# Statistics of the second image: 32 pieces of 512 pixels in three pairs a period, in place of 64 pieces of 256 spread over it

## The chip, the cores and the metric

The kernel runs on one core of a Trainium2 chip. The metric is the device time of one launch in microseconds (us), as the median of several runs. Profiles show one execution of the program; DVE is VectorE, ACT ScalarE, PE TensorE, POOL GpSimd, and SP the engine whose queue issues nearly all the DMAs here.

## What is computed

The input `x` is float32, 2 images x 512 channels x 64 x 64 pixels. There are two layers with a residual each:

```python
x = x + _L0_conv_ref(_gn(x), ...)   # group norm, then deformable convolution
x = x + _L1_conv_ref(_gn(x), ...)   # group norm, then attention over 4096 pixels
```

Layer 0 normalizes each image over 32 groups of channels (`_gn`: mean and variance of a group over all its pixels). A projection of the normalized image is the source that is sampled. A depthwise 3x3 convolution, a layer norm over channels and a GELU give, by a matmul, offsets and masks; bilinear samples at the offset places, weighted by the masks, go through an output matmul. So nothing of the second image can be projected before the mean and the variance of that whole image are known: this is what `image_stats` supplies.

## The kernel before

An image is cut into 8 chunks of 512 pixels (`CH = 512`, `NCH = 8`, 8 rows of 64), the channels into 4 blocks of 128 partitions (`KB = 4`). Layer 0 is a software pipeline over 16 chunks (`NSEQ = 16`, 8 of each image). The stages are generators, and each `yield` ends a step:

- `project(i)` (L724) reads chunk i of x into `raw` (three of the four loads in its first step, L737), normalizes it on ACT into `xn` (L748), multiplies it by the input weights (`pq`, L758) and writes the rows to DRAM (`xt<-xj`, L766).
- `features(i)` (L771): the first of nine taps of the depthwise convolution on ACT (L783), the other eight of each channel block on DVE (L788, 32 instructions), the sum over blocks on POOL (L796), the mean over channels by a matmul (`p_mean`, L801), the subtraction on DVE (L806), squares, the root of the variance on ACT (`rstd`, L818), then the norm: its reciprocal (L820) and the product (L821) on DVE, and GELU on ACT (L825).
- `weights(i)` (L833): offsets and masks (`po` on PE L842, `o` on DVE L847), then the bilinear weights on DVE (L859 to L890), a copy on ACT (L893) and transposes.
- `sample(i)` (L919): matmuls (`pb`, `pa`) on patches of projected pixels, the output matmul `py` (L969), and its evacuation on DVE: an addition (L974), a bn_stats for layer 1 (L975) and a write of the chunk (`wx<-res`, L976). At the end of each half of `pa`, `fetch` (L905 to L916) issues eight loads of patches for the next chunk (L914, 192 KB each).
- `image_stats(1)` (L697): one step per piece of the second image. It keeps up to three loaded pieces in `xraw` (three buffers): each step first issues loads until three pieces are under way, then takes the oldest for a `bn_stats` (L713) on DVE. The load of piece k+2 is therefore issued in the step of piece k. After a channel block's last piece, at the start of the following step, comes a `bn_aggr` (L715). The group norm's few instructions follow (`group_norm_steps`, L599).

The order of all this is written out by hand in `period` (L998 to L1050), which is called 16 times inside `tc.manual_schedule()` (L1087): on every engine, and in SP's queue of DMAs, instructions stand in the order in which `period` resumes the generators. Its letters: `y` is `sample(i-1)` in its output part, `v` and `w` the weights of chunks i and i+1, `f` the features of i+2, `m` `sample(i)`, `g` the features of i+3 (its ACT tap only), `p` the projection of i+3, and `more` one step of `image_stats(1)`. A period starts with `p(); y(); v(4); f(4); y()`: raw loads, first output matmul, transposes, four taps, evacuation. Then four rounds of `m(2); w(); more(); f(taps); w(); more()` do the other 28 taps. The mean follows, outputs, and the step `f()` of the norm (L820, L821) after `p(); y(2)`. The tail of the period has the products of `weights`, the projection's matmuls and writes, and five more `more()`. A period so has 13 steps of `more`, five periods 65: the 64 pieces and the last `bn_aggr`. At i = 5 (`NCH - 3`), `run(later)` (L1091) finishes the statistics, since period 5 projects chunk 8, the first of the second image.

Image 0's statistics use the same function ahead of the periods (with pieces of 512, from tiles that hold the whole image).

Layer 1 (attention) follows and takes the rest of the span.

Of the kernel before, what the change touches and what calls it, by code (L numbers as in the profile page):

```python
# [9 lines left out]
F32 = mybir.dt.float32  # L10
# [7 lines left out]
P = 128  # L18
NB = 2
C = 512  # L20
KB = C // P
H = W = 64
S = H * W
# [7 lines left out]
CH = 512  # L31
NCH = S // CH
# [498 lines left out]
def kernel(ctx: ExitStack, tc: tile.TileContext, t_in: dict, out: bass.AP):  # L531
# [7 lines left out]
    nc.vector.tensor_reduce(al[:, 1:2], al[:, 0:1], AX.X, ALU.max, apply_absolute_value=True)  # L539
    nc.vector.memset(al[:, 0:1], 1.0 / SCORE_MAX)  # L540
    window_path(tc, t_in, out, far, sums)


# [27 lines left out]
def window_path(ctx: ExitStack, tc: tile.TileContext, t_in: dict, out: bass.AP, far: bass.AP, sums: bass.AP):  # L571
    nc = tc.nc
    x_v = t_in["x"].rearrange("n (cb p) h w -> n p cb (h w)", p=P)
# [25 lines left out]
    def group_norm_steps(mv, k, small, psum, result):  # L599

        p1 = psum.tile([P, CH], F32, tag="mm", name="gn_p1")
        nc.tensor.matmul(p1[:, : 2 * k], gmat, mv.rearrange("p k s -> p (k s)"), start=True, stop=True)
        yield
        gm = small.tile([P, k, 2], F32, name=f"gn_gm{k}")
        nc.vector.tensor_copy(gm.rearrange("p k s -> p (k s)"), p1[:, : 2 * k])
        d = small.tile([P, k], F32, name=f"gn_d{k}")
        nc.vector.tensor_sub(d, mv[:, :, 0], gm[:, :, 0])
        nc.vector.tensor_mul(d, d, d)
        yield
        p2 = psum.tile([P, CH], F32, tag="mm", name="gn_p2")  # L610
        nc.tensor.matmul(p2[:, :k], gmat, d, start=True, stop=True)
        yield
        var = small.tile([P, k], F32, name=f"gn_var{k}")
        nc.vector.tensor_add(var, gm[:, :, 1], p2[:, :k])
        nc.scalar.activation(var, var, AF.Sqrt, bias=eps)
        yield
        sc = small.tile([P, k], F32, name=f"gn_sc{k}")
        nc.vector.reciprocal(sc, var)
        bi = small.tile([P, k], F32, name=f"gn_bi{k}")
        nc.vector.scalar_tensor_tensor(bi, gm[:, :, 0], -1.0, sc, ALU.mult, ALU.mult)  # L620
        result += [sc, bi]
# [8 lines left out]
    with ExitStack() as l0:  # L630
        wp = l0.enter_context(tc.tile_pool(name="w0w", bufs=1))
        io = l0.enter_context(tc.tile_pool(name="w0io", bufs=1))
        cv = l0.enter_context(tc.tile_pool(name="w0conv", bufs=1))
        sm = l0.enter_context(tc.tile_pool(name="w0small", bufs=1))
# [10 lines left out]
        img = [bt.rearrange("p g q d -> p (g q d)")[:, h * S : (h + 1) * S] for h in range(2)]  # L645
# [51 lines left out]
        def image_stats(n):  # L697

            mv = sm.tile([P, KB, 2], F32, name="gn_mv")
            size = CH if n == 0 else CH // 2  # L700
            pieces, ahead = deque((kb, h) for kb in range(KB) for h in range(S // size)), deque()
            for kb in range(KB):
                st = sm.tile([P, 16, 6], F32, name="gn_st")
                for h in range(S // size):
                    if n == 0:
                        t = img[kb][:, h * size : (h + 1) * size]
                    else:
                        while len(ahead) < 3 and pieces:
                            k2, h2 = pieces.popleft()
                            ahead.append(io.tile([P, size], F32, name="xraw", bufs=3))  # L710
                            nc.sync.dma_start(ahead[-1], x_v[n, :, k2, h2 * size : (h2 + 1) * size])
                        t = ahead.popleft()
                    nc.vector.bn_stats(st[:, h, :], t)  # L713
                    yield
                nc.vector.bn_aggr(mv[:, kb, :], st[:, : S // size].rearrange("p a b -> p (a b)"))  # L715
            yield
            result = []
            yield from group_norm_steps(mv, KB, sm, ps, result)
            sc, bi = result
            gn[n] = [sm.tile([P, KB], F32, name=f"gn_{k}{n}") for k in ("scale", "bias")]  # L720
            nc.vector.tensor_copy(gn[n][0], sc)
            nc.vector.tensor_copy(gn[n][1], bi)
# [184 lines left out]
        def fetch(i, s):  # L907

            if i >= NSEQ:
                return  # L910
            n, ch = divmod(i, NCH)
            t = io.tile([P, PX, C], F32, name="patch", bufs=2)
            for p in range(PX):
                nc.sync.dma_start(  # L914
                    t[:SN, p, :], xt_d[n][ch * ROWS + PR * s : ch * ROWS + PR * s + SY, PC * p : PC * p + SX, :]
                )  # L916
            patches[i, s] = t
# [61 lines left out]
        def run(*generators):  # L979
            for gen in generators:  # L980
                for _ in gen:
                    pass
# [15 lines left out]
        def period(y, v, m, w, f, g, p, more):  # L998

            p()
            y()
            v(4)
            f(4)
            y()
            for taps in (9, 7, 6, 6):
                m(2)
                w()  # L1010
                more()
                f(taps)
                w()
                more()
            w()
            m()
            w()
            m()
            f()
            y()  # L1020
            f()
            m()
            p()
            w(2)
            y(2)
            w()
            m()
            p()
            f()
            w(2)  # L1030
            p()
            y(2)
            f()
            y()
            m()
            p()
            more()
            for k, steps in enumerate((1, 2, 2, 2)):
                p()
                w(steps)  # L1040
                if k == 0:
                    f()
                p()
                more()
                if k < 3:
                    m()
                if k == 0:
                    f()
                if k == 2:
                    g()  # L1050
            w()
# [17 lines left out]
        def output_bias():  # L1069
# [8 lines left out]
            yield  # L1078

        run(image_stats(0), project(0), value_weights(), features(0), project(1))  # L1080
        v = Chain(weights, 0)
        v(23)
        run(features(1), project(2), output_bias())
        fetch(0, 0)
        fetch(0, 1)
        later, y, f = image_stats(1), Chain(sample, NSEQ), Chain(features, 2)
        with tc.manual_schedule():  # L1087
            f()
            for i in range(NSEQ):
                if i == NCH - 3:  # L1090
                    run(later)  # L1091
                w, m, g = Chain(weights, i + 1), Chain(sample, i), Chain(features, i + 3)
                period(y, v, m, w, f, g, Chain(project, i + 3), lambda: next(later, None))
                y, v, f = m, w, g
            y.rest()

# [4 lines left out]
    with ExitStack() as l1, tc.manual_schedule():  # L1101
# [8 lines left out]
        with ExitStack() as at, ExitStack() as inner:  # L1110
# [69 lines left out]
            mv = bnp.tile([P, NB * KB, 2], F32, name="mv2")  # L1180
# [107 lines left out]
            for n in range(NB):  # L1288
# [38 lines left out]
                for qb in range(NCH):  # L1327
                    acc = {}
                    for kp in range(NPAIR + 2):
# [23 lines left out]
                        if kp < NPAIR:  # L1353
                            v = ready.pop(0)
                            e, tt, _ = made[qb, kp]
                            ops = operands(lambda k: e[:, k, :], tt)
                        else:
                            v = w7[:, kp - NPAIR]
# [17 lines left out]
                    a = [acc[j].rearrange("p (cb q) -> p cb q", cb=2) for j in range(6)]  # L1376
# [156 lines left out]
```

## Time and profile before

| | us |
|---|---|
| median of three runs | 3704.61 (3700.99 to 3706.11) |
| the profiled execution | 3707.44 |
| its span, first to last instruction | 3705.6 |
| first tap of period 1 to that of period 2, of 2 to 3, of 3 to 4 | 75.3, 75.9, 74.7 |

| engine | busy us | share of the span |
|---|---|---|
| PE | 3417.9 | 92% |
| DVE | 2345.8 | 63% |
| ACT | 1304.1 | 35% |
| POOL | 291.0 | 8% |

The mean granted TensorE clock is 0.968 of full speed. The profile is read in several views: the page's 40 slices of the span with busy tenths; the waits, in which a line gives the instruction that waited, the one that released it, the total in us, the count and the longest; the timeline, in which each line is a start, a duration, an engine, a source line and an operation, with the idle time before it in brackets; the issues on SP's queue (SPq), which show when a DMA was issued and not when it landed; and the chain that ended last, followed back from the end, in which a DMA has the time from its issue to its landing.

In the traced execution the 64 pieces of `xraw` run on DVE from 175.1 to 533.0 us, 403 to 429 ns each, 25.8 us in all with their overlap. Image 0's 32 pieces of 512 take 675 to 694 ns each.

### The profile page before, as it was taken

The numbers are of one execution on the slowest core, as the hardware profiler recorded it, in microseconds if no ns is written. First come the engines' busy times: TensorE is split into PE (matmuls) and PEld (weight loads), VectorE is DVE, ScalarE is ACT, GpSimd is POOL, SyncE is SP. The second block draws the span as 40 slices with busy tenths as digits, with TensorE's granted clock in tenths as the row PEclk, the third lists the DMA queues.
The fourth block names the chain that finished last, engine by engine and source line by source line (L and its number), as shares of the span: only waits on it lengthen the run. The fifth ranks groups of instructions, "written<-read, shape, count | busy, mean of one in ns | idle before, by whom it ended". The sixth has DMA issues, their size and how long they took to land.

```text
span 3705.6 us, 39010 instructions
## 1 busy us (share of the span) xinstructions
PE 3417.9 (92%) x15151; PEld 2433.8 (66%) x15151; DVE 2345.8 (63%) x3575; ACT 1304.1 (35%) x1691; POOL 291.0 (8%) x190
## 2 busy tenths in 40 slices
PE   4689998999998799999999999999999999999990
PEld 1355555555555477777777777777777777777770
DVE  5798989999996475545554554567455455545544
ACT  2476777787886321111111111221111111111114
POOL 2112111212111030000000000022000000000000
PEclk9789999999999899999999999999999999999995
DMA  7233442342432444334334333444433333243349
GB/s 240 63 98 114 135 137 83 115 133 83 127 109 78 142 157 171 126 129 139 123 108 163 122 125 130 140 155 169 149 121 111 122 138 111 101 149 121 111 162 389
DMA packets 180181, 500.06 MB, mean 135 GB/s; under 512 B 22640, under 2 KB 64368, under 8 KB 170512
## 3 DMA queue, kind: packets, MB, share of 16 engines
q1 hardware_dynamic: 176496, 473.34, 37.5%
q10 hardware_dynamic: 3456, 24.12, 1.7%
q8 instruction: 121, 1.98, 0.2%
q14 instruction: 76, 0.62, 0.0%
q0 software_dynamic: 32, 0.00, 0.0%
HBM read 406.09 MB, written 91.29 MB: 134 GB/s over the span
## 4 chain that ended last, share of the span: by engine, by line
PE 75%; DVE 15%; DMA 4%; ACT 2%; SPq 1%; issue 1%; POOL 1%; ACTq 0%; DVEq 0%; POOLq 0%
PE acc L1364 41%; DVE conv L788 8%; PE pS L1211 7%; PE p L1402 7%; PE py L969 5%; PE pq L758 4%; PE pa L949 4%; PE pv L1251 3%; PE pk L1305 1%; PE p_mean L801 1%; DVE pk L885 1%; DVE aw L890 1%; DMA patch<-xt 1%; DMA out<-ct 1%; DVE o L847 1%
## 5 line engine op out<-in xcount | busy, mean ns | idle before, releaser
L1364 PE MATMUL acc<-e,v 128*128 128x256 f32 x3072 | 768.2, 386 | 0.0
L1215 ACT ACTIVATE e<-pS 128x1024 f32<-128x1024 f32 x256 | 262.0, 1024 | 1386.4 <-PE pS L1211 1313.0
L1364 PE MATMUL acc<-tt,v 128*128 128x256 f32 x3072 | 748.2, 380 | 0.5 <-DMA v<-wv 0.5
L1364 PEld LDWEIGHTS acc<-e,v 128*128 128x128 f32 x3072 | 566.5, 190 | 233.2 <-issue 165.3
L1364 PEld LDWEIGHTS acc<-tt,v 128*128 128x128 f32 x3072 | 582.4, 190 | 91.2 <-issue 10.6
L1218 DVE TENSOR_TENSOR t<-e 128x256 f32<-128x256 f32 x256 | 108.8, 425 | 761.1 <-ACT e L1215 761.1
L788 DVE SCALAR_TENSOR_TENSOR conv<-xn,L_conv_dw_w_sb,conv 128x504 f32<-128x504 f32 (+1 forms) x512 | 399.7, 795 | 48.5 <-ACT conv L783 36.5
L1228 DVE TENSOR_TENSOR tot<-tot,e 128x512 f32<-128x512 f32 x480 | 330.1, 688 | 8.3
L949 PEld LDWEIGHTS pa<-bt,patch 96*128 96x128 f32 x2048 | 251.8, 197 | 63.1 <-issue 39.4
L1211 PE MATMUL pS<-q,kq 64*128 64x512 f32 x1024 | 289.0, 641 | 0.0
L949 PE MATMUL pa<-bt,patch 96*128 96x128 f32 x2048 | 255.3, 281 | 9.3 <-ACT dT L960 5.8
L935 ACT COPY bt<-pb 96x1024 f32<-96x1024 f32 x124 | 234.2, 2001 | 58.9 <-PE pb L930 58.9
L758 PE MATMUL pq<-L_conv_in_w_sb,xn 128*128 128x512 f32 x512 | 236.3, 605 | 4.3 <-ACT xn L748 4.3
L969 PE MATMUL py<-dT,L_conv_out_w_sb 128*128 128x512 f32 x512 | 238.0, 610 | 0.0
L1402 PE MATMUL p<-t,v 128*128 128x256 f32 x1024 | 231.4, 382 | 1.7 <-DMA v<-wv 1.7
L1402 PEld LDWEIGHTS p<-t,v 128*128 128x128 f32 x1024 | 192.1, 190 | 48.5 <-issue 21.2
L960 ACT COPY dT<-pa 32x256 f32<-32x256 f32 x496 | 179.5, 362 | 89.8 <-PE pa L949 80.9
L842 PE MATMUL po<-om_w_pg,feat 128*128 128x432 f32 x512 | 203.4, 542 | 0.0
L969 PEld LDWEIGHTS py<-dT,L_conv_out_w_sb 128*128 128x128 f32 x512 | 99.3, 197 | 119.6 <-issue 115.5
L758 PEld LDWEIGHTS pq<-L_conv_in_w_sb,xn 128*128 128x128 f32 x512 | 94.1, 194 | 109.5 <-issue 93.0
L842 PEld LDWEIGHTS po<-om_w_pg,feat 128*128 128x128 f32 x512 | 93.0, 191 | 90.5 <-issue 89.4
L1211 PEld LDWEIGHTS pS<-q,kq 64*128 64x128 f32 x1024 | 77.1, 184 | 84.9 <-issue 84.9
(203 smaller groups left out, 3731.2 us busy)
## 6 DMA issues: line engine op xcount, KB each, us to landing
v<-wv SPq DMA_DIRECT2D x252, 768.0 KB
patch<-xt SPq DMA_DIRECT2D x256, 192.0 KB
v<-wv SPq DMA_DIRECT2D x256, 128.0 KB
wv<-v SPq DMA_DIRECT2D x32, 896.0 KB
xt<-xj SPq DMA_DIRECT2D x128, 128.0 KB
res<-in_x SPq DMA_DIRECT2D x64, 256.0 KB
wx<-res SPq DMA_DIRECT2D x64, 256.0 KB
xq<-wx SPq DMA_DIRECT2D x16, 1024.0 KB
```

The lines of the kernel that those rows point to most:

```text
L758: nc.tensor.matmul(pq, xn[:, kb, 1 + 2 * t : 3 + 2 * t, :].rearrange("p r c -> p (r c)"), in_w[:, kb, :], start=(kb == 0), stop=(kb == KB ...
L788: nc.vector.scalar_tensor_tensor(dst, src, wt, dst, ALU.mult, ALU.add)
L842: nc.tensor.matmul(po[:, : 3 * GP], f[:, kb, t * P : (t + 1) * P], om_w[:, kb].rearrange("p a k g -> p (a k g)"), start=(kb == 0), stop=(k ...
L935: copy(bt[:SN].rearrange("s g q d -> s d (g q)")[:, d0 : d0 + 4, :], pb[:SN])
L949: nc.tensor.matmul(pa[:, p], xp[:SN, p, cb * P : (cb + 1) * P], bt[:SN, 4 * cb : 4 * cb + 4, PX * s + p, :], start=True, stop=True,)
L960: copy(dst, src)
L969: nc.tensor.matmul(py, out_w[:, kb, cb * P : (cb + 1) * P], dT[:, kb, :], start=(kb == 0), stop=(kb == KB - 1))
L1211: nc.tensor.matmul(pS[:, h, :], kq[r, 2 * (kp // 4) + h, c0 : c0 + P], qs[qb][r, :], start=True, stop=True)
L1215: nc.scalar.activation(e.rearrange("p a q -> p (a q)"), pS.rearrange("p h q -> p (h q)"), AF.Exp)
L1228: nc.vector.tensor_add(tots[qb], tots[qb], e2[:, h, :])
L1364: nc.tensor.matmul(acc[j][:, cb * HQ : (cb + 1) * HQ], v[:, j, cb * P : (cb + 1) * P], ops[j], start=(kp + cb == 0), stop=(kp + cb == NPAI ...
L1402: nc.tensor.matmul(p7[:, cb * HQ : (cb + 1) * HQ], v7[:, cb * P : (cb + 1) * P], t3, start=(k + cb == 0), stop=(k + cb == NPAIR + 2),)
```

## The change

`image_stats(1)` uses pieces of 512 pixels (256 KB a load in place of 128 KB), 32 in place of 64, still with three buffers. `more` takes a number of pieces. The 13 single steps of a period go; there are three pairs in their place: ahead of the first four taps, between these and the output's evacuation, and ahead of the norm. That is 6 steps a period and 30 in five, so `run(later)` at period 5 has two pieces and a `bn_aggr` more to do. Image 0's statistics are the same as before.

```diff
         def image_stats(n):
 
             mv = sm.tile([P, KB, 2], F32, name="gn_mv")
-            size = CH if n == 0 else CH // 2
-            pieces, ahead = deque((kb, h) for kb in range(KB) for h in range(S // size)), deque()
+            pieces, ahead = deque((kb, h) for kb in range(KB) for h in range(NCH)), deque()
             for kb in range(KB):
-                st = sm.tile([P, 16, 6], F32, name="gn_st")
-                for h in range(S // size):
+                st = sm.tile([P, NCH, 6], F32, name="gn_st")
+                for h in range(NCH):
                     if n == 0:
-                        t = img[kb][:, h * size : (h + 1) * size]
+                        t = img[kb][:, h * CH : (h + 1) * CH]
                     else:
                         while len(ahead) < 3 and pieces:
                             k2, h2 = pieces.popleft()
-                            ahead.append(io.tile([P, size], F32, name="xraw", bufs=3))
-                            nc.sync.dma_start(ahead[-1], x_v[n, :, k2, h2 * size : (h2 + 1) * size])
+                            ahead.append(io.tile([P, CH], F32, name="xraw", bufs=3))
+                            nc.sync.dma_start(ahead[-1], x_v[n, :, k2, h2 * CH : (h2 + 1) * CH])
                         t = ahead.popleft()
                     nc.vector.bn_stats(st[:, h, :], t)
                     yield
-                nc.vector.bn_aggr(mv[:, kb, :], st[:, : S // size].rearrange("p a b -> p (a b)"))
+                nc.vector.bn_aggr(mv[:, kb, :], st.rearrange("p a b -> p (a b)"))
             yield
...
             p()
             y()
             v(4)
+            more(2)
             f(4)
+            more(2)
             y()
             for taps in (9, 7, 6, 6):
                 m(2)
                 w()
-                more()
                 f(taps)
                 w()
-                more()
             w()
...
             p()
             y(2)
+            more(2)
             f()
             y()
             m()
             p()
-            more()
             for k, steps in enumerate((1, 2, 2, 2)):
                 p()
                 w(steps)
                 if k == 0:
                     f()
                 p()
-                more()
                 if k < 3:
                     m()
...
         later, y, f = image_stats(1), Chain(sample, NSEQ), Chain(features, 2)
+
+        def more(pieces):
+
+            for _ in range(pieces):
+                next(later, None)
+
         with tc.manual_schedule():
...
-                period(y, v, m, w, f, g, Chain(project, i + 3), lambda: next(later, None))
+                period(y, v, m, w, f, g, Chain(project, i + 3), more)
```

## The prediction

> **What bounds the kernel now.** I read the page's 40 slices first, to find the stage the change touches. A digit is the busy tenth of 92.6 us.
>
> ```profile
> PE   4689998999998799999999999999999999999990
> DVE  5798989999996475545554554567455455545544
> ```
>
> DVE is at 9 tenths up to about slice 12, PE from slice 14 on. The change touches only layer 0's first six periods, where both are close to full, so I went to the waits of DVE between 171 and 545 us (periods 0 to 4, and the start of 5).
>
> ```profile
> DVE conv L788 <- ACT conv L783: 10.5, 4, 8.0
> DVE rstd L820 <- ACT rstd L818: 10.2, 5, 3.1
> DVE gn_st L713 <- DMA xraw<-in_x: 8.7, 5, 2.9
> DVE res L974 <- PE py L969: 5.7, 4, 1.4
> ```
>
> These are the three places of the new calls (first taps L788, evacuation L974, norm L820), and a wait of the statistics on their own loads. Third, DVE's timeline where period 1 begins (start, duration, in brackets the idle time before).
>
> ```profile
> 236.76 0.43 DVE L713 BATCH_NORM_STATS2 gn_st<-xraw 128x6 f32<-128x256 f32 x1 [0.82 <-DMA xraw<-in_x]
> 238.58 3.09 DVE L788 SCALAR_TENSOR_TENSOR conv<-xn,L_conv_dw_w_sb,conv 128x504 f32<-128x504 f32 x4 [1.39 <-ACT conv L783]
> 243.09 0.75 DVE L974 SCALAR_TENSOR_TENSOR res<-py,L_conv_out_b_sb,res 128x512 f32<-128x512 f32 x1 [1.42 <-PE py L969]
> ...
> 244.81 6.85 DVE L788 SCALAR_TENSOR_TENSOR conv<-xn,L_conv_dw_w_sb,conv 128x504 f32<-128x504 f32 x9
> ...
> 254.13 0.43 DVE L713 BATCH_NORM_STATS2 gn_st<-xraw 128x6 f32<-128x256 f32 x1 [1.62 <-DMA xraw<-in_x]
> ```
>
> The four first taps end at 241.67; a piece issued at the first `more()` of the period is waited for at 254.13. Fourth, SP's issues over the same stretch, and the chain's step through it.
>
> ```profile
> 236.64 0.54 SPq L711 DMA_DIRECT2D xraw<-in_x  x1
> 237.24 0.42 SPq L941 DMA_DIRECT2D res<-in_x  x1
> 237.75 5.67 SPq L914 DMA_DIRECT2D patch<-xt  x8
> 243.52 1.14 SPq L766 DMA_DIRECT2D xt<-xj  x2
> 244.75 0.53 SPq L711 DMA_DIRECT2D xraw<-in_x  x1
> 245.40 2.40 SPq L737 DMA_DIRECT2D raw<-in_x  x3
> 248.63 0.33 SPq L976 DMA_DIRECT2D wx<-res  x1
> ```
> ```profile
> 242.77 6.99 DMA patch<-xt
> 249.77 4.33 DMA xraw<-in_x
> 254.13 0.43 DVE gn_st L713
> ```
>
> This is the view that decides. At a period's edge SP issues eight patch loads (192 KB each), two xt writes and three raw loads (320 KB each); the last patch has landed at 249.75, and the piece issued behind all that needs 4.33 us more, where the piece issued at 234.35 took 2.39. The chain that sets the end runs through it.
>
> **What the Trainium skill says.** *DMA: Bandwidth & Descriptors*, section Queues, rings and completion order: SP's transfers share one row of rings, and each DMA engine takes descriptors in ring order. The trace agrees: 4.33 against 2.39 us. *Perfetto Trace Analysis*, section DMA Instruction — HWDGE: the profiled stretch of an issue is not the movement of the data; so I take landings from the chain, not from the 0.33 us of an issue. *VectorE: DVE Perf Modes*, section on the TRN2 errata: every instruction on SBUF operands pays a fixed cost (58 cycles at 0.96 GHz, 60 ns), so larger pieces pay it less often. The trace agrees: eight 512-wide bn_stats of image 0 take 4.84 us, 0.605 each; a pair of 256-wide ones 0.74, a pitch of 0.333. Two halves cost 0.666, one whole 0.605: 0.061 saved.
>
> **The change part by part.**
>
> *Size of the piece.* 64 x 0.333 = 21.3 us become 32 x 0.605 = 19.4: 2 us of DVE in all. The transfers double to 256 KB, the total is the same.
>
> *Number of pieces.* Before, 13 `more()` a period, 65 by the end of period 4: 64 pieces and the last bn_aggr. After, 6 a period: 30. The last two pieces and a bn_aggr fall to `run(later)` at the head of period 5. There, DVE has shed four trailing pieces of period 4 (4 x 0.335 = 1.3 us) and gets 2 x 0.605 = 1.2; the group norm then waits 4.7 us on ACT L615 anyway. I take 0, bounds -1 and +1.
>
> *Issue order, the heart of it.* Each resumption tops `ahead` up to three, then uses the oldest: piece k issues the load of k+2. Call a period's pairs A (before the first taps), B (after four taps), C (before the norm). A's two resumptions issue B's loads, B's issue C's, C's issue the next A's. So A and C arrive early: C's loads have 40 us, the next A's some 20. B's loads are issued at the head of the period, behind eight patches, two xt and three raw, and are wanted four taps later. Before, the load issued at the first `more()` was used two resumptions on, nine taps and an evacuation later, and still came 1.34 to 2.87 us late.
>
> *When B lands.* Let T0 be the start of the first tap (238.58, 313.91, 389.82, 464.54 for periods 1 to 4). The reference load landed just before its bn_stats, at 254.13, 330.71, 405.81, 479.82: T0 + 15.6, 16.8, 16.0, 15.3, mean 15.9. Bytes behind the patches up to there: xt 0.26, xraw 0.13, raw 0.98, wx 0.26, xraw 0.13 MB, 1.77 in all. After, to the end of b1: xt 0.26, raw 0.98, b1 0.26, 1.5 MB; to the end of b2 1.77, the same. The DMA moves about 0.385 MB/us there (356 to 397 GB/s in the slices before 250), so b1 lands 0.7 before b2. Three of the trailing xraw issues stood in SP's chain ahead of the patches, and two of them between an xt and a res, at 0.59 each: the patches start about 1 us earlier. b2: T0 + 14.9; b1: T0 + 14.2.
>
> *What that costs.* Four taps end at T0 + 3.1. DVE then idles to T0 + 14.2, 11 us, since the instruction at its head waits. Queued behind it: the evacuation and its bn_stats (1.4), 28 taps, the om additions, the sum for the mean. Behind the evacuation waits the x1 write on SP, behind the taps POOL and then PE's p_mean. b2 ends at T0 + 15.5; evacuation and stats 1.4, nine taps 6.8, addition 0.5 bring it to T0 + 24.2. Before, the same point, third `more()` included, is at T0 + 16.2. Loss 8.0. Five later `more()` before the mean go: 5 x 0.335 = 1.7. Net 6.3 a period, 25 us over four periods.
>
> *Is it given back later?* From p_mean to the norm the chain is PE (py, pa, py, pa: 277.04 to 289.6), then ACT, queued in order behind p_mean; it moves as a whole. Pair C costs 1.2 and lies in the wait for rstd (0.9 to 3.1), I take 0; uncovered it would be 1.2 x 4 = 5 us. Pair A (1.2) takes the place of two of the trailing pieces and of the 0.5 to 1.4 us wait on ACT's L783; T0 is set by ACT, so 0, both ways at most 1.3 a period. The `c2` load waits on SP for bn_stats of b1; behind it only the x1 write, which waits for the same DVE: 0.
>
> *Period 0.* Its first three loads are issued at 140.6, long before use. Eight `more()` go (2.7 us), B costs 1.2, C 0.3 beyond a wait of 0.9: -1.2. But b2 waits for a1's buffer and may stand behind the xt writes, which end at 176.3; with 2.4 + 0.35 for landing it comes at 179, DVE wants it at 175.3: up to +3.8. I take +1, bounds -1.2 and +2.6.
>
> Sum: 25 + 1 = +26 us. The profiled execution took 3707.4 us (span 3705.6, 1.8 around it), the median is 3704.6, the runs spread over 5. On the profiled one: 3733; on the median: 3730.6, given as 3730.
>
> **Rivals.**
>
> *B's loads pass the bulk.* The patches keep the DMA engines only half busy (digits 4 to 6 in that stretch), so b1 and b2 might land 2.7 us after their issue, at about T0 + 11 and T0 + 11.7. Then the nine taps end at T0 + 21: loss 4.8 - 1.7 = 3.1 a period, 12 in all: 3717. Against it: the same traffic held the reference load for 4.33 us.
>
> *Faster: the pairs do fit into the gaps.* If b1 and b2 were there when the four taps end, DVE would reach the point of comparison at T0 + 3.1 + 1.2 + 1.4 + 6.8 + 0.5 = T0 + 13.0 in place of 16.2, and save 1.7 more: 4.9 a period, 20 in four, 1 in period 0: 3684. It decides from the landing of b2: sooner than T0 + 8.6 is a gain, later a loss. Against it: the eighth patch, ahead in the same queue, lands at T0 + 11.2.
>
> *Worse: nothing of the 1 us on SP is gained, and C and A lie open.* Each period 1 + 1.2 + 1 more: +13: 3743.
>
> *No change to speak of:* the idle DVE lets PE and ACT run ahead, so that the waits of 10.2 (rstd) and 5.7 (py) go, together with the early landing: 3707. Against it: what PE does between p_mean and rstd stands behind p_mean.
>
> **How the numbers follow.** Main case 0.74, 3730, own range 3720 to 3741. Early landing 0.11, 3717. Worse 0.05, 3743. No change 0.05, 3707. Faster 0.05, 3684. The range 3712 to 3744 leaves out the last two and the tails. 0.2% is 7.4 us, about what a measurement of this kernel can tell from no change. Faster by more (under 3697): 0.05. Within: 0.05 and 0.03 of the early landing's lower side, 0.08. Slower: 0.87.
>
> **What would show it.** In periods 1 to 4 DVE should wait some 11 us in front of the first bn_stats after four taps, released by DMA xraw; the wait of L713 on xraw rises from 8.7 to about 44 to 48 us. The waits of L974 on PE (5.7) should vanish, those of L820 shrink by C. A period from first tap to first tap goes from 75.3 to about 81.6 us; from period 6 on nothing changes. If L713's wait stays under 20 us, the landing is wrong; if it is there and the periods don't grow, the step "not given back" is wrong.

## The result and the profile after

The changed kernel takes 3730.12 us (3727.86 to 3730.84, four runs) against 3705.36 us (3700.99 to 3706.92): a ratio of 1.007, 95% interval 1.0058 to 1.0082. It is 24.8 us slower; 3730 was forecast. Between the two profiled executions the difference is 22.8 us (3730.26 against 3707.44).

Below, A, B and C are a period's three pairs: ahead of the first four taps, behind them, and ahead of the norm. The waits of DVE in the changed kernel, over the same periods (165 to 568 us; source lines are one or a few lower than before; total us, count, longest):

```profile
DVE gn_st L712 <- DMA xraw<-in_x: 44.8, 4, 11.9
DVE conv L787 <- ACT conv L782: 11.6, 5, 7.6
...
DVE rstd L819 <- ACT rstd L817: 2.8, 4, 1.5
```

The wait for the statistics' own loads went from 8.7 us to 44.8, four waits of 10.8 to 11.9 us. The evacuation's wait on PE (5.7 before) is gone, and the norm's wait on ACT went from 10.2 to 2.8: the pairs at B and C do lie where DVE had been idle, as the change's placement means them to. But the wait ahead of B costs far more than the pairs cover. DVE at the head of period 1, in the changed kernel:

```profile
233.34 1.28 DVE L712 BATCH_NORM_STATS2 gn_st<-xraw 128x6 f32<-128x512 f32 x2
237.23 3.09 DVE L787 SCALAR_TENSOR_TENSOR conv<-xn,L_conv_dw_w_sb,conv 128x504 f32<-128x504 f32 x4 [2.60 <-ACT conv L782]
240.23 0.37 DVE L714 BATCH_NORM_AGGREGATE gn_mv<-gn_st 128x2 f32<-128x48 f32 x1
251.50 1.31 DVE L712 BATCH_NORM_STATS2 gn_st<-xraw 128x6 f32<-128x512 f32 x2 [10.90 <-DMA xraw<-in_x]
252.72 0.73 DVE L973 SCALAR_TENSOR_TENSOR res<-py,L_conv_out_b_sb,res 128x512 f32<-128x512 f32 x1
...
254.10 6.85 DVE L787 SCALAR_TENSOR_TENSOR conv<-xn,L_conv_dw_w_sb,conv 128x504 f32<-128x504 f32 x9
```

Pair A (233.34) finds its data there. Pair B waits from 240.6 to 251.5, and the evacuation (L973) and the next nine taps, which before ran in this time, stand behind it. SP's queue and the chain of the changed kernel over the same stretch give the reason:

```profile
235.54 5.65 SPq L913 DMA_DIRECT2D patch<-xt  x8
241.29 1.14 SPq L765 DMA_DIRECT2D xt<-xj  x2
242.47 2.03 SPq L736 DMA_DIRECT2D raw<-in_x  x3
245.26 7.28 SPq L710 DMA_DIRECT2D xraw<-in_x  x4
```
```profile
239.14 6.06 DMA patch<-xt
...
245.26 6.14 DMA xraw<-in_x
251.50 1.31 DVE gn_st L712 x2
```

B's first load goes out at 245.26, 8 us after the first tap; its data are there 6.1 us later. DVE wanted it 3.1 us after the first tap. Both parts are long: the last load of the same period, issued at 252.22 with almost nothing ahead of it, took 2.7 us for the same 256 KB.

The chain shows what the issue waited for: the sixth patch load had to land (239.14 and 6.06 us; the issue follows after 0.06). The semaphores in the trace tell why. From the head of period 1 to B's loads each DMA signals its landing on one of eight semaphores, in turn, and so shares one with the DMA eight issues earlier; none starts before that one has landed. B's first load is the sixth behind the last patch and so waits for the sixth patch, its second for the seventh. SP's own waits in this stretch (236 to 258 us) show it for three of the four loads and for a raw load:

```profile
SPq L710 <- DMA patch<-xt: 2.7, 3, 1.0
...
SPq L736 <- DMA patch<-xt: 0.6, 1, 0.6
```

**Where the 23 us are.** From first tap to the subtraction of the mean (L805 after, L806 before), periods 1 to 4 take 45.3, 46.0, 45.4 and 45.0 us, and took 38.9, 40.3, 38.8 and 38.0: +25.6 in sum. From there to the norm they take 15.3, 15.7, 16.2, 14.9 against 16.6, 15.7, 16.1, 14.9: -1.2. From the norm to the next first tap nothing changed (19.85 both). The first tap of period 1 comes 1.35 sooner; 1.04 of this is there at the first tap of period 0 already, where profiles differ by as much with the same instructions ahead of it (170.52 in the changed kernel, 171.69 in e2 below). In sum +23.0, and that is what stands at the norm of period 6 (685.10 against 662.05). From there to the norms of period 13 each period takes 67.7 us in both.

One thing is needed for the comparisons below. From the norm of period 13 to the last evacuation of layer 0 the profiles take one of two times: 140.8 to 140.9 us in the kernel before, the changed kernel and e2, and 136.5 to 136.9 us in the nine others. The granted TensorE clock differs with it: in the kernel before, the chain of matmuls that DVE waits for there lay in 7 us at a mean of 0.63, in e4 the same chain lay in a stretch at 1.00; a later stretch at 0.50 lasts 27.3 us in the three profiles and 17.1 in the nine. What makes an execution take the one or the other is open. So a kernel is read in two numbers: its median, and the time of the norm of period 6 in its profile, which lies ahead of that stretch. Of the second, differences of about 1 us may mean nothing (the first tap of period 0 lies at 170.0 to 172.3 us in the twelve profiles).

### The profile page after: what moved, and what is told of

The parts are those of the page before. It is cut to its first block, busy times and chain, and to the rows that moved or that the text cites. A ratio compares the mean times of both kernels' runs of the same rounds, so it can differ in the third digit from the quotient of the medians.

```text
span 3728.1 us, 38946 instructions
## 1 busy us (share of the span) xinstructions
PE 3415.9 (92%) x15151; PEld 2433.1 (65%) x15151; DVE 2349.3 (63%) x3543; ACT 1305.0 (35%) x1691; POOL 292.8 (8%) x190
## 4 chain that ended last, share of the span: by engine, by line
PE 74%; DVE 16%; DMA 4%; ACT 1%; issue 1%; SPq 1%; POOL 1%; ACTq 0%; DVEq 0%; POOLq 0%
PE acc L1368 41%; DVE conv L787 9%; PE pS L1215 7%; PE p L1406 6%; PE py L968 5%; PE pv L1255 4%; PE pq L757 4%; PE pa L948 4%; PE pk L1309 1%; DVE pk L884 1%; DVE aw L889 1%; DMA patch<-xt 1%; PE p_mean L800 1%; DMA out<-ct 1%; DVE o L846 1%
## 5 line engine op out<-in xcount | busy, mean ns | idle before, releaser
L948 PE MATMUL pa<-bt,patch 96*128 96x128 f32 x2048 | 254.5, 281 | 9.3 <-ACT dT L959 5.8
```

What stands on the lines that cost most here:

```text
L948: nc.tensor.matmul(pa[:, p], xp[:SN, p, cb * P : (cb + 1) * P], bt[:SN, 4 * cb : 4 * cb + 4, PX * s + p, :], start=True, stop=True,)
```

## The experiments

Each kernel was timed in rounds beside the kernel before on the same chip. The kernel before had a median of 3705.4 us beside the changed kernel, 3702.4 beside e1 to e4, 3703.3 beside e5 to e8, and 3705.4 beside e9 and e10; so kernels of different groups are compared by their difference from it. All times are in us.

| run | median | against before | ratio to before, 95% interval | norm of period 6, against before |
|---|---|---|---|---|
| the changed kernel | 3730.1 | +24.8 | 1.0058 to 1.0082 | +23.0 |
| e1, pair A's steps ahead of the raw loads | 3714.0 | +11.6 | 1.0021 to 1.0048 | +15.5 |
| e2, pair B after nine taps | 3693.2 | -9.1 | 0.9965 to 0.9986 | -6.4 |
| e3, load k+3, pieces 2, 2, 2 | 3725.4 | +23.1 | 1.0049 to 1.0077 | +21.4 |
| e4, load k+3, pieces 2, 1, 3 | 3678.2 | -24.2 | 0.9920 to 0.9947 | -22.3 |
| e5, B's loads on ACT's queue | 3733.1 | +29.9 | 1.0068 to 1.0095 | +26.8 |
| e6, pairs at C, tail, A | 3676.4 | -26.9 | 0.9915 to 0.9942 | -27.5 |
| e7, before, load k+3 | 3690.1 | -13.2 | 0.9952 to 0.9979 | -11.4 |
| e8, as e4, pieces of 256 | 3680.8 | -22.5 | 0.9925 to 0.9952 | -22.7 |
| e9, pair A ahead of the patches | 3680.6 | -24.8 | 0.9923 to 0.9950 | -25.9 |
| e10, as e6, load k+3 | 3674.8 | -30.6 | 0.9907 to 0.9934 | -29.6 |

### e1: the order on SP alone

```diff
+            more(2)
             p()
             y()
             v(4)
-            more(2)
             f(4)
             more(2)
```

> Pair A stands ahead of p() in place of behind v(4); DVE's order is the same, only on SP do the two loads of pair B now stand ahead of the three raw loads (0.98 MB). Theory (B's loads are queued behind the bulk at the head of the period): at 0.385 MB/us they land 2.5 us sooner, DVE's wait on xraw falls from 44.8 to about 35 us, and the time from 3730 to about 3720 us. Rival (a 256 KB load is slow by itself, or the place of the pair on DVE costs the time): within 2 us of the changed kernel's 3730.

Measured: 3714.0 us, 11.6 over the kernel before where the changed kernel is 24.8 over it; at the norm of period 6 it is 7.5 under the changed kernel, of which 6.5 is the wait (44.8 to 38.3 in periods 1 to 4). In the profile another 4.2 us lie in the last two periods, with the clock. DVE's order is the same; only the place of two loads among SP's issues moved. In the profile the first goes out 6.1 us after the first tap of period 1 in place of 8.0 (at 242.53 in place of 245.26), and the wait in period 1 is 8.63 in place of 10.90. So the order of issue matters, by 2.3 us in that period where 2.5 was expected, by 1.1 to 1.8 in the others. The wait fell less than expected (to 38, not to 35), and most of it is still there, with the patches still ahead.

### e2: the place of the pair on DVE

```diff
             f(4)
-            more(2)
             y()
...
                 f(taps)
                 w()
+                if taps == 9:
+                    more(2)
```

> Pair B moves from behind the first four taps to behind the evacuation, the next nine taps and the first offset addition; its loads are issued where they were. Theory: the loads still land 14 to 15 us after the first tap, but DVE has work until 13.2 us: a wait of about 1 us a period is left in place of 11, 5 in all, and the wait on py (5.7) comes back; time about 3695. Rival (the waits come from pairs of large pieces as such, each second load waiting for the first one's buffer): the wait moves with the pair and stays near 40 us, time about 3730.

Measured: 3693.2 us, 9.1 under the kernel before. The wait on xraw is 7.8 us in four waits, where 5 was expected, and the evacuation's 5.7 on PE is back, as expected. The loads are as late as they were, 14.1 to 16.1 us after the first tap; DVE has its 10 us of work first. The rival (pairs wait for one another's buffers) falls.

### e3 and e4: the load one piece earlier

```diff
+            def top_up():
+                while len(ahead) < 3 and pieces:
...
                     else:
-                        while len(ahead) < 3 and pieces:
...
+                        top_up()
                         t = ahead.popleft()
                     nc.vector.bn_stats(st[:, h, :], t)
+                    if n:
+                        top_up()
                     yield
```

Behind each bn_stats its buffer is refilled at once, so piece k issues the load of k+3. e3 has only this; e4 has `more(2)`, `more(1)`, `more(3)` at A, B, C as well.

> Buffers are topped up behind each bn_stats too, so that piece k issues the load of k+3 in place of k+2; still three buffers, pairs where they were. The first load of B is now issued in pair C of the period before, early; the second still at the head of the period, behind the patches and raw loads. Theory: the wait moves to B's second piece and stays, shorter only by B's first 256 KB (0.7 us): wait 42 to 44 us, time about 3727. Rival (B's first load is the late one): wait under 10, time about 3690.

> As the run before, but with pieces 2, 1, 3 at the three places in place of 2, 2, 2: now all loads of A and B are issued in C of the period before, those of C at the head of the period, 40 us ahead of use. Theory: no wait on xraw is left (under 2 us); the piece at B lies in the wait on py, C's third piece costs at most 0.6 us a period: time about 3687, faster than the kernel before. Rival (the place between the first taps and the evacuation costs the time, whatever the loads do): 3720 or more.

Measured: e3 3725.4 us, wait 42.1; e4 3678.2 us, no wait on xraw at all. In e3, DVE at the head of period 1:

```profile
237.86 3.09 DVE L793 SCALAR_TENSOR_TENSOR conv<-xn,L_conv_dw_w_sb,conv 128x504 f32<-128x504 f32 x4 [2.67 <-ACT conv L788]
...
241.26 0.70 DVE L716 BATCH_NORM_STATS2 gn_st<-xraw 128x6 f32<-128x512 f32 x1
251.59 0.69 DVE L716 BATCH_NORM_STATS2 gn_st<-xraw 128x6 f32<-128x512 f32 x1 [9.62 <-DMA xraw<-in_x]
```

The first piece of B, loaded in the period before, runs at once; the second, whose load still goes out at the head of the period, waits nearly as long. The same place in e4, where the one piece of B was loaded in the period before:

```profile
237.51 3.09 DVE L793 SCALAR_TENSOR_TENSOR conv<-xn,L_conv_dw_w_sb,conv 128x504 f32<-128x504 f32 x4 [2.17 <-ACT conv L788]
...
240.92 0.70 DVE L716 BATCH_NORM_STATS2 gn_st<-xraw 128x6 f32<-128x512 f32 x1
242.02 0.75 DVE L979 SCALAR_TENSOR_TENSOR res<-py,L_conv_out_b_sb,res 128x512 f32<-128x512 f32 x1 [0.41 <-PE py L974]
```

The statistics lie in the evacuation's wait on PE, of which 0.41 us of 1.42 is left: the three places the change chose are good, given the data. e4 beat its expectation by 9 us; 3 of these are the kernel before, faster in this group. Some 4 are the stretch with the clock. And the first tap of the next period follows the norm of periods 1 to 3 after 19.13, 19.14 and 19.54 us in place of 19.85: that stretch was taken as fixed by ACT, and is not quite.

### e5: another queue

```diff
-                            nc.sync.dma_start(ahead[-1], x_v[n, :, k2, h2 * CH : (h2 + 1) * CH])
+                            queue = nc.scalar if (k2 * NCH + h2) % 6 in (2, 3) else nc.sync
+                            queue.dma_start(ahead[-1], x_v[n, :, k2, h2 * CH : (h2 + 1) * CH])
```

> The changed kernel with only the two loads of each pair B issued from ACT's queue, at the same place in the order of the program (on ACT behind the copies of the transposes, some 9 us after the first tap; on SP they went 8 us after it). They leave the row of the patches and raw loads. Theory of the order (what is late is their place behind the bulk in SP's row): they land about 2.7 us after the issue, DVE's wait falls by 2 to 3 us a period, from 44.8 to about 35, time about 3720. Rival (the DMA engines are full at that moment, whatever the row): wait as before within 3 us, time 3728 to 3732.

A miss for the theory as it stood: 3733.1 us and a wait of 48.9. In periods 1 to 4 the wait is 45.0, as in the changed kernel (44.8); the other 3.9 are in period 0, where the loads on ACT's queue go out at 174 us, some 30 us later than on SP. In period 1 of e5 B's first load goes out 7.6 us after the first tap and is there 6.7 us after its issue, no sooner than on SP's row. What the DMA engines moved between 249 and 254.5 us in e5 (the queue, its packets, MB, share of the 16 engines; the first line is the engines' busy tenths):

```profile
DMA  9897557989899999898897899989698998988889
...
q1 hardware_dynamic: 561, 1.17, 65.6%
q10 hardware_dynamic: 283, 0.52, 29.0%
```

Both rows ran side by side (q10 is ACT's). The engines were nearly full, and B's 0.52 MB took all of 5.5 us. So "their place behind the bulk in one row" is not the mechanism. What is left: they were issued late, and while the bulk was under way in the engines that both rows use.

Two things limit what e5 can say. It leaves the time of issue as it was (7.6 us after the first tap, 8.0 before), and it doesn't free it from the patches: ACT's DMAs take their turn on the same eight semaphores, and B's second load, out at 249.87, has that of the sixth patch, which landed at 249.78. No run gives B's loads semaphores of their own, so what this wait costs apart from their place in the order is open. And the bulk and B's loads land in the order of their issue across the two rows: raw 254.21, B 254.42, raw 255.70, B 255.92, raw 256.51.

### e9: ahead of the patches

```diff
             v(4)
-            more(2)
             f(4)
             more(2)
...
+                if k == 2:
+                    more(2)
                 if k < 3:
                     m()
```

> The changed kernel with pair A moved into the tail of the period, ahead of the step that issues the second eight patch loads; pair B stays between the first four taps and the evacuation, still three buffers and the load of k+2. B's loads now go out on SP ahead of the patches. After the run with B's loads on ACT, what is left of the theory is: a load is late that is issued while the bulk is under way, whatever its row; it is on time if it is issued ahead. So: no wait on xraw over 1 us a period, time 3677 to 3687. Rival (256 KB loads take 6 us or more at the edge of a period wherever they are issued): a wait of 3 us or more a period, time 3695 or more.

Measured: 3680.6 us; 4.0 us of waits on xraw: 1.24 and 0.15 at B's second piece in periods 2 and 3, and 2.60 in the two last pieces at period 5. The 1.24 is over the 1 us a period that was expected, but of 44.8 us of waiting at B 1.4 are left. Still three buffers, still the load of k+2, still a pair of 512 at B. SP and DVE in period 1 of e9:

```profile
235.78 1.01 SPq L710 DMA_DIRECT2D xraw<-in_x  x2
...
237.35 5.67 SPq L913 DMA_DIRECT2D patch<-xt  x8
```
```profile
238.09 3.09 DVE L787 SCALAR_TENSOR_TENSOR conv<-xn,L_conv_dw_w_sb,conv 128x504 f32<-128x504 f32 x4 [2.81 <-ACT conv L782]
241.09 1.28 DVE L712 BATCH_NORM_STATS2 gn_st<-xraw 128x6 f32<-128x512 f32 x2
```

Issued 1.6 us ahead of the patches, the loads are there when B starts, 5.3 us later. In period 2, the worst of the four, the second load went out at 306.39, 0.9 us ahead of the patches, and took 5.0 us:

```profile
309.47 0.69 DVE L712 BATCH_NORM_STATS2 gn_st<-xraw 128x6 f32<-128x512 f32 x1
311.39 0.69 DVE L712 BATCH_NORM_STATS2 gn_st<-xraw 128x6 f32<-128x512 f32 x1 [1.24 <-DMA xraw<-in_x]
```

So a load ahead of the burst is slowed by it too: B's loads take 3.4 to 5.1 us in e9, 5.1 to 6.3 in the changed kernel. The larger gain is the time of issue. In periods 1 to 4 B's first load goes out 1.1 to 2.3 us ahead of the first tap in place of 8.0 to 8.6 us behind it. Together with e1 and e3 this settles the cause: B's loads are late because they are issued behind the patches (and, for a smaller part, the raw loads). Of the 12 us that they land sooner in period 1, 10 are the earlier issue and 2 the shorter way.

### e6, e7, e8 and e10: what else there was to have

e6 takes pair B out of the front, into the tail of the period (`if k == 1: more(2)`), with the loads as in the changed kernel; e10 adds the refill. e7 is the kernel before with only the refill. e8 is e4 with pieces of 256, twice as many and in six buffers of half the size.

> Three buffers and the load of k+2 as in the changed kernel, but pair B stands in the tail of the period (behind the second round of weights) and nothing between the first taps and the evacuation. Every pair's loads are then issued well ahead of the bulk or well ahead of use. Theory: wait on xraw under 4 us; the tail pair lies open (1.2 us a period over the run with pieces 2, 1, 3): time about 3684. Rival (any use of 512-wide pairs keeps a stall of some us): 3695 or more.

> The kernel before (13 single pieces of 256 a period) with only the refill behind each bn_stats: piece k issues the load of k+3. Theory: the load wanted at the third step of a period is now issued ahead of the raw loads, the wait of 8.7 us on xraw is gone or under 2: time some 7 us under the kernel before. Rival (those waits are hidden behind PE and ACT anyway): within 2 us of the kernel before.

> The run with refill and pieces 2, 1, 3 a period, with pieces of 256 pixels in place of 512: 4, 2, 6 at the same places, six buffers of half the size, so the same bytes are loaded at the same places. It isolates the size of a piece. By the pitches (0.333 and 0.605 us) DVE has 2 us more to do, part of it in the waits on ACT and py: 1 to 2 us slower than the run with 512. Rival (the size carries the gain): 5 us or more slower.

> The run with pairs at the norm, in the tail and ahead of the first taps, plus the refill behind each bn_stats (piece k issues the load of k+3). The 3.1 us of waits on xraw that were left there should go: about 3673, against 3676 without the refill; if these waits lie beside ACT's, no change.

Measured: e6 3676.4 us with 3.1 us of waits on xraw, 8 under its expectation: the 1.2 us a period for the tail's pair don't show (26.9 under the kernel before, e4 24.2). e7 3690.1 us, 13 under the kernel before where 7 were expected. Its 8.7 us of waits on xraw are gone, and at the norm of period 6 it is 11.4 ahead; how much of the 13 is the clock can't be told from one profile. So the kernel before had the same fault in small. e8 is 22.5 under the kernel before, e4 24.2; the intervals overlap, and at the norm of period 6 they are level (-22.7 and -22.3). The 1 to 2 us expected for the size of the piece are not shown, and it doesn't carry the gain. e10 3674.8 us: 1.0 us of waits left, the lowest median, but its interval (0.9907 to 0.9934) overlaps e6's (0.9915 to 0.9942).

## Why the prediction was right, step by step

- **Issue order and the stall.** Forecast: B lands at 14.2 us after the first tap, DVE idles 11 us, waits of 44 to 48 us. Measured: 14.3, 15.0, 14.4 and 13.9 us; idle 10.9, 11.9, 11.3, 10.8; 44.8 in sum. The second load lands 0.65 to 0.68 us behind the first, where 0.7 was expected. (These and other landings are the last of a load's updates on its semaphore in the trace.)
- **The reason for the landing.** The sum of bytes behind the patches gave the right time, since at B the DMAs land in the order of their issue. But its picture of one row in ring order, taken from *DMA: Bandwidth & Descriptors*, section Queues, rings and completion order, doesn't carry: in e5 another row brought nothing. The same page's section Issuing engines are not separate DMA queues says that DMAs from different engines run on the same 16 DMA engines and interleave; e5's trace agrees (0.52 MB of q10 in 5.5 us beside 1.17 MB of q1). That section would have been the one to build on. What the prediction did not read in its own view is that SP waits for the patches: its reference load went out at 249.77, 0.02 us after the eighth patch, eight issues earlier, had landed.
- **The loss in the front of a period.** Forecast 6.3 us, 25 in four; measured 25.6.
- **Nothing given back later.** Forecast 0; measured -1.2, once, in period 1. PE's work behind the mean moved as a whole, as argued.
- **Period 0.** The term that was wrong in sign: +1 forecast. From the first tap of period 0 to that of period 1 the changed kernel is 0.3 us shorter (66.71 against 67.02), 1.35 with what lies ahead of it. The load that was feared to be late wasn't: pair A of period 0 ran at 145.6 us, in a gap 25 us ahead of the first tap, so that five loads were out by 148 us and B had no wait.
- **Where luck helped.** The sum, +26, is 3 us too high against the profiles (+23.0 at the norm of period 6), from the two terms above. The median rose by 24.8, so that 3730 fits it better than the terms do; a difference of 2 us between medians and single profiles is within the spread of the runs (6 us for the kernel before).
- **run(later), and SP's start of the patches.** Forecast 0 and 1 us earlier. From the norm of period 4 to the group norm's reciprocal (L618) 27.0 us in both; against the first tap the patches start 0.6 to 1.3 us sooner (in period 1, 1.69 us ahead of it in place of 0.83).
- **Rivals.** The faster one, pairs that fit into the gaps, has its price confirmed by e4 and e9: 20 us under the kernel before forecast for data that are there in time, 24.2 and 24.8 measured. It failed on what was held against it, the landing.

## What to carry to other kernels

A step that uses what an earlier step loads has two places: where it computes, and where its predecessor issues its load. Moving the step moves both, and the second can land behind a burst of other transfers, where a load of 256 KB went out 8 us late and took 6 us in place of 2.7; look at the queue's issues around the new place, and at what they wait for, before moving anything. Still with three buffers, issuing B's loads ahead of the burst (e9), or moving the pair to where its loads are in time (e6), turned +25 us into -25 and -27. Refilling right behind the use (the load of k+3) is no cure by itself: with the pairs left as they were it gained 2 us (e3), with one piece at B 49 (e4).

## What was not expected of the hardware

Giving the late loads a row of their own (ACT's queue) did not bring them sooner while the DMA engines were busy: 6.7 us from issue to use against 6.2 on SP's row. Nor did it make their issue independent of SP's: in this program the DMAs of both queues share eight semaphores, and an issue waits until the DMA eight before it has landed. And the last two periods of layer 0, where DVE waits for PE, take 140.8 or 136.5 us in profiles of kernels that do the same there, together with the granted TensorE clock (0.63 in the kernel before and 1.00 in e4 over the matmuls waited for).
